# GroupNorm statistics of two residual sums from accumulating additions and ScalarE's squares instead of VectorE's bn_stats

## The chip, the cores and the metric

The kernel runs on one core of one Trainium2 chip. A core has TensorE (PE, matrix products), VectorE (DVE), ScalarE (ACT), GpSimd (POOL) and SyncE (SP, which here only issues DMAs); each works through its own queue of instructions in order, and they wait for each other by semaphores. The metric is the device time of one execution in microseconds, of which the median of several runs counts.

## The reference, cut to what matters

Four layers run one after the other on x of 16 x 32 x 128 x 128 fp32 (batch, channels, rows, columns). Each takes the GroupNorm of x (16 groups of two channels) and adds its result to x.

```
def _gn(v, G=16, eps=1e-5):
    g = v.reshape(B_, G, C_ // G, H_, W_)
    m = jnp.mean(g, axis=(2, 3, 4), keepdims=True)
    s = jnp.var(g, axis=(2, 3, 4), keepdims=True)
    return ((g - m) / jnp.sqrt(s + eps)).reshape(v.shape)
...
x = x + _L0_conv_ref(_gn(x), ...)    # a scan of LSTM cells over 128 columns
x = x + _L1_conv_ref(_gn(x), ...)    # quantised; out = -sum over c,kh,kw of |patch - w|
x = x + _L2_conv_ref(_gn(x), ...)    # Hartley transform, 32 x 32 modes mixed over channels, back
x = x + _L3_conv_ref(_gn(x), ...)    # five edge filters, seven 3x3 convolutions, three upsamplings
```

The means and variances that layers 2 and 3 need are those of x after layer 1 and after layer 2. This is what the change computes in another way.

## The kernel before, in words

**Stage 0** (`stage0`, to about 687 us) is layer 0. It already takes the statistics of its own result, for layer 1, from additions with a sum (L191, a custom VectorE operation followed by a read of the accumulator) and from squares on ScalarE (L198, with an accumulator read).

**The front** (`Differences.run`, L682) is layer 1. Work goes by half images: 16 batches x 2 halves, each a unit of 72 *differences* (8 output groups x 9 taps). A difference is max(q - w, 0) over a tile of 128 x 8192 fp16, made either by VectorE (L760, tile `d_dve`, three buffers) or by ScalarE (L757, tile `d_act`, two buffers). TensorE adds each up over partitions into four PSUM banks (`sums`, L647, 16 matmuls of 512 columns), together with a linear part (L662) and, where the plan leaves it idle, matmuls with zeros (`keep_busy`, L677). When a unit is complete, `finish` (L624) adds the four banks to the residual `xr1` (four scalar_tensor_tensor, L628), takes bn_stats of each (L630), and later stores the sum as x2 (eight DMAs).

**The background** (`After`) is layers 2 and 3. It works on groups of four batches. Group g starts when batch 4g+3 has been finished: `scaling` (L1149) aggregates the bn_stats of its four batches; `forward` does the Hartley transform (L1107 to L1083), reflects and mixes the modes (L1218); `back` (L1245) transforms back (L1292, L1342) and in 16 steps adds the result to the residual (`take_out`: two scalar_tensor_tensor, L1317, two bn_stats, L1320), which lies in `xr2` in a ring of four buffers: a step is stored as x3, and the buffer is loaded again for the step four later (`residual`, L1261). After the last step `back` aggregates the 32 bn_stats (L1359) and forms the mean and scale of layer 3 (`normalised`, L780). Then come the filters' statistics (L1488), conv1 (L1871), the small layers (L1661, L908) and the last layer (`last`, L1923, additions at L1993).

**The order of the work** is written out ahead by a planner, `Weave`, and kept as it stands (`keep_order`). The planner carries a clock for each engine, `weave.dve`, `weave.act` and `weave.pe`, to which each step adds its cost (`DVE_US, ACT_US, PE_US = 2.36, 7.15, 0.88` for a difference on VectorE, on ScalarE, and its sums on TensorE). Each next difference goes to the engine that would end it first (L742 to L749). Steps put off with `later(us, step)` are issued when the plan's time has reached them; `summed(step)` puts one off until after the matmuls planned so far; `done(v)` issues one at once if it still waits. A negative number that a generator yields is a distance that the plan keeps before the next step.

Groups 0 to 2 run in the background of the front. What is left of group 2, and all of group 3, run in **the tail**, where `drain` (L455) interleaves the two. Group 3 has the whole image in SBUF (`self.whole`), so that its way back adds in place and neither stores nor reloads.

Of the kernel before, what the change touches and what calls it, by code (L numbers as in the profile page):

```python
# [333 lines left out]
def by_rows(nc, tile, dram, store=False):  # L334

    for j in range(4):
        part = tile[32 * j : 32 * j + 32]
        rows = bass.AP(dram.tensor, dram.offset + j * dram.ap[0][0], [list(v) for v in dram.ap[1:]])
        if store:
            nc.sync.dma_start(rows, part)  # L340
        else:
            nc.sync.dma_start(part, rows)


def jc_rows(t, b, half, at=0, rows=16):

    first = t.offset + b * CHW + (64 * half + at) * W
    return bass.AP(t.tensor, first, [[16 * W, 4], [HW, C], [1, rows * W]])


class Weave:
# [103 lines left out]
def drain(*weaves):  # L455

    live = list(weaves)
    for w in live:
        w.draining, w.stretch = True, 1.5
    while live:  # L460
        w = min(live, key=lambda w: w.now)
        us = w.step()
        w.now = max(w.now + (us or 0.0), w.until)
        w.due(float("inf") if us is None else w.now)
        if us is None:
            live.remove(w)
            for w in live:
                w.alone, w.stretch = True, 1.0


def keep_order(nc, tc, start):

    last = {}
    for i in nc.cur_bb.bb.instructions[start:]:
        if i.engine in last:
            tc.add_manual_dep(
                i,
                last[i.engine].name,
                mybir.DependencyInfo(mybir.DependencyClass.NoSync, mybir.DependencyReason.DATA),
                reason="order",  # L480
            )
        last[i.engine] = i

DVE_US, ACT_US, PE_US = 2.36, 7.15, 0.88
LATE, ACT_SPARE = 1.5, 1.5
SLACK, CLOCK = 1.0, 1.0
# [3 lines left out]
def rest(nc, tc, cst, sel16, bias, m1, r1, a, d, out):  # L493


    with ExitStack() as ctx:
        sm = ctx.enter_context(tc.tile_pool(name="s1_sm", bufs=1))
        stat = sm.tile([128, B, 8, 6], F32, name="stat2")
        with tc.tile_pool(name="s1_ps0", bufs=2, space=PSUM) as ps:
            first = Differences(nc, sm, ps, cst, sel16, m1, r1, a["adder_w"], d, stat)  # L500
        bg = ctx.enter_context(tc.tile_pool(name="b_ps", bufs=4, space=PSUM))
        after = After(nc, tc, "left", sm, bg, cst, bias, a, d, stat, out)
        weave = after.weave = Weave(after.work(range(NG - 1)))
        start = len(nc.cur_bb.bb.instructions)
        with ExitStack() as front:
            first.run(tc, front, weave)
        keep_order(nc, tc, start)

        end = copy.copy(after)
        end.side, end.ps = "right", ctx.enter_context(tc.tile_pool(name="c_ps", bufs=4, space=PSUM))  # L510
        end.spare, end.whole = bg, True

        end.buffers = {"t_x": 8, "xm": 8, "xw": 4, "t_w": 6, "t_r": 8, "frames": 3, "gm": 5, "e_v": 6, "l_x": 4}
        end.weave = Weave(end.work([NG - 1]))
        end.weave.now = end.weave.base = weave.now
        end.weave.finished = B - 1
        drain(weave, end.weave)


class Differences:  # L520
# [103 lines left out]
    def finish(self, b, half, acc, xr, **_):  # L624
        nc = self.nc
        v = [xr[k // 2][:, 512 * (k % 2) : 512 * (k % 2) + 512] for k in range(4)]
        for k in range(4):
            nc.vector.scalar_tensor_tensor(v[k], acc[k], self.sumw, v[k], ALU.subtract, ALU.add)  # L628
        for k in range(4):
            nc.vector.bn_stats(self.stat[:, b, 4 * half + k, :], v[k])  # L630

        def store():
            for i in range(2):
                by_rows(nc, xr[i], jc_rows(self.d["x2"], b, half, 8 * i, 8), True)
            if half:
                self.weave.finished = b

        start = max(self.weave.dve, self.weave.pe)
        self.weave.pe, self.weave.dve = start + 2.6, start + 5.6
        self.weave.later(max(self.weave.dve - self.weave.base, 0.0) + 0.5, store)  # L640

    def sums(self, acc, d, i, first, last):
# [320 lines left out]
class After:  # L963
# [185 lines left out]
    def scaling(self, g, pool):  # L1149

        nc, cst, weave = self.nc, self.cst, self.weave
        mr = self.sm.tile([128, 2, 4, C], F32, name="mr", bufs=2)
        mv = pool.tile([128, 4, 2], F32, name="mv2")
        for i in range(4):
            nc.vector.bn_aggr(mv[:, i, :], self.stat[:, 4 * g + i].rearrange("p a b -> p (a b)"))
        both = pool.tile([128, 2, 4], F32, name="both2")
        yield from normalised(nc, pool, self.ps, weave, mv, 4, cst["avg8_jc"], 1e-5, both)

        diag = pool.tile([32, 8, C], F32, name="diag")
        nc.vector.tensor_tensor(  # L1160
            diag, bcast(cst["ident"][:32, :], 1, 8), bcast(both[:32].rearrange("p a b -> p (a b)"), 2, C), ALU.mult
        )
# [82 lines left out]
    def back(self, g, load):  # L1245


        nc, tc, cst, d, weave = self.nc, self.tc, self.cst, self.d, self.weave
# [3 lines left out]
        with self.pool("t_z") as zp_, self.pool("t_r", ahead) as rp:  # L1252
# [10 lines left out]
            def in_place(n, r):  # L1263

                row = 2 + 64 * (n % 2) + 32 * r + 4 * (n // 2)
                return self.image[:, row : row + 4, 2 : W + 2]

            xr = []
            stat = zp_.tile([128, 32, 6], F32, name="stat3")
            zi = zp_.tile([128, 32, 32], F32, name="zi")  # L1270
            for blk in range(4):
                first = z_d.offset + (4 * g + blk) * 32768
# [13 lines left out]
            for oh in range(2):  # L1286
                pa = [self.acc() for _ in range(4)]
                for o in range(16):
                    for r in range(4):
                        for blk in range(4):  # L1290
# [5 lines left out]
                                start=True,  # L1296
# [13 lines left out]
            def take_out(n, pf):  # L1310
                while ready.get(n):
                    weave.done(ready[n])
                for r in range(2):
                    v, p = xr[n][:, r] if not self.whole else in_place(n, r), pf[r]
                    if self.whole:
                        p = p.rearrange("p (r w) -> p r w", w=W)
                    nc.vector.scalar_tensor_tensor(v, p, 2.0**-15, v, ALU.mult, ALU.add)  # L1317
                for r in range(2):
                    v = xr[n][:, r] if not self.whole else in_place(n, r)
                    nc.vector.bn_stats(stat[:, 2 * n + r, :], v)  # L1320
                weave.dve += 2.8
                if self.whole:
                    return

                def store():
                    nc.sync.dma_start(rows(n)(x3), xr[n])
                    ready[n + ahead] = weave.later(6.0, lambda: reload(n + ahead)) if n + ahead < 16 else None

                ready[n + ahead] = weave.later(4.0, store)

            def reload(n):
                residual(n)
                ready[n] = None

            previous = None
            for n in range(16):
                s, half = n // 2, n % 2
                pf = [self.acc() for _ in range(2)]
                for i in range(4):
                    for r in range(2):  # L1340
# [5 lines left out]
                            start=True,  # L1346
# [8 lines left out]
            take_out(*previous)  # L1355
            if not self.whole:
                weave.later(7.0, lambda: [load(ch, half) for ch in range(self.buffers["frames"]) for half in range(2)])
            mv = zp_.tile([128, 1, 2], F32, name="mv3")
            nc.vector.bn_aggr(mv[:, 0, :], stat.rearrange("p a b -> p (a b)"))  # L1359
            yield from normalised(nc, zp_, self.ps, weave, mv, 1, cst["avg2_bc"], 1e-5, self.stats3)  # L1360
            nc.vector.scalar_tensor_tensor(
                self.shift3, self.stats3[:, 0], -1.0, self.stats3[:, 1], ALU.mult, ALU.mult
# [804 lines left out]
```

## Time and profile before

| | us |
|---|---|
| median of three runs | 6466.08 (6465.73 to 6471.06) |
| the profiled execution | 6473.52 |
| its span in the trace | 6471.7 |
| first difference starts, last sums end | 687.3, 5630 |
| VectorE, ScalarE, TensorE busy over the span | 5455.2, 5276.5, 5326.5 |
| differences on VectorE, on ScalarE | 1674, 630 |
| bn_stats at L630 and at L1320 | 128 and 128 |

The profile comes from one execution. Times are us, and those of single instructions often ns. An instruction's duration can overlap the next one's start on the same engine by about 0.1 us, so two equal instructions in a row tell their cost better by the distance between their starts. A wait is put down to what ended it last. "Idle before" in a group's row is the engine's idle time just before instructions of the group. In the list of differences by shape, 8192 and 8320 columns are two tilings of the same work.

### The profile page before, as it was taken

The numbers are of one execution on the slowest core, as the hardware profiler recorded it, in microseconds if no ns is written. First come the engines' busy times: TensorE is split into PE (matmuls) and PEld (weight loads), VectorE is DVE, ScalarE is ACT, GpSimd is POOL, SyncE is SP. The second block draws the span as 40 slices with busy tenths as digits, with TensorE's granted clock in tenths as the row PEclk, the third lists the DMA queues.
The fourth block names the chain that finished last, engine by engine and source line by source line (L and its number), as shares of the span: only waits on it lengthen the run. The fifth ranks groups of instructions, "written<-read, shape, count | busy, mean of one in ns | idle before, by whom it ended". The sixth has DMA issues, their size and how long they took to land.

```text
span 6471.7 us, 275922 instructions
## 1 busy us (share of the span) xinstructions
PE 5326.5 (82%) x130160; PEld 2805.8 (43%) x130160; DVE 5455.2 (84%) x6528; ACT 5276.5 (82%) x2779; POOL 58.7 (1%) x67
## 2 busy tenths in 40 slices
PE   3689577788877879998877879998888699977696
PEld 3576233344434433334443433334344333345594
DVE  7899899999999989999999889999999899834212
ACT  3899799999999989999999879999999899702001
POOL 0000000000000000000000000000000000000000
PEclk9999899999999989999999989999999899977898
DMA  7643313121154633222455532323455522344102
GB/s 313 222 178 125 87 48 84 48 57 45 32 138 124 204 117 88 64 72 73 142 147 150 168 93 58 97 51 102 129 144 179 162 58 63 97 131 137 33 4 65
DMA packets 363701, 700.94 MB, mean 108 GB/s; under 512 B 67972, under 2 KB 216452, under 8 KB 351684
## 3 DMA queue, kind: packets, MB, share of 16 engines
q1 hardware_dynamic: 355092, 648.86, 33.6%
q0 software_dynamic: 7040, 33.80, 1.6%
q8 instruction: 1018, 16.68, 1.1%
q14 instruction: 119, 0.97, 0.1%
q10 hardware_dynamic: 432, 0.64, 0.0%
HBM read 500.46 MB, written 182.69 MB: 106 GB/s over the span
## 4 chain that ended last, share of the span: by engine, by line
PE 26%; issue 11%; DVE 8%; ACT 3%; DMA 2%; SPq 0%; POOL 0%; DVEq 0%; ACTq 0%; POOLq 0%
PE acc L1871 10%; PE acc L647 9%; DVE d_dve L760 4%; PE acc L908 3%; ACT d_act L757 2%; PE acc L1661 1%; PE acc L1488 1%; PE acc L1292 1%; DMA xm_d<-xm 0%; PE acc L1218 0%; PE acc L662 0%; DVE pooled L1764 0%; PE acc L934 0%; DMA v<-fold_d 0%; PE acc L1844 0%
## 5 line engine op out<-in xcount | busy, mean ns | idle before, releaser
L757 ACT ACTIVATE d_act<-q,neg 128x8192 f16<-128x8192 f16 (+1 forms) x630 | 4463.6, 7152 | 215.9 <-PE acc L647 197.4
L760 DVE TENSOR_SCALAR d_dve<-q,qw 128x8192 f16<-128x8192 f16 (+1 forms) x1674 | 3868.3, 2360 | 215.3 <-PE acc L647 193.1
L647 PE MATMUL acc<-d_dve,sel 128*32 128x512 f16 x26784 | 1850.6, 395 | 409.4 <-DVE d_dve L760 305.6
L647 PEld LDWEIGHTS <-sel 128*32 128x32 f16 x36864 | 983.9, 99 | 1934.0 <-issue 1265.0
L647 PE MATMUL acc<-d_act,sel 128*32 128x512 f16 x10080 | 708.5, 401 | 147.9 <-ACT d_act L757 140.8
L1871 PE MATMUL acc<-xp,wf 32*32 32x512 f32 x19200 | 725.4, 607 | 23.0 <-issue 21.5
L677 PE MATMUL acc<-q,zero 128*32 128x512 f16 x8396 | 576.7, 390 | 7.1 <-issue 7.0
L223 PE MATMUL pg<-h,wb 64*64 64x20 f32 (+15 forms) x8192 | 341.3, 304 | 61.6 <-DVE h L251 34.8
L908 PE MATMUL acc<-y,u_conv 32*32 32x256 f32 x10752 | 318.4, 435 | 60.7 <-issue 45.1
L237 ACT ACTIVATE gt<-pg,bias 128x20 f32<-128x20 f32 (+15 forms) x1024 | 331.5, 383 | 41.6 <-PE pg L223 39.7
L1871 PEld LDWEIGHTS acc<-xp,wf 32*32 32x32 f32 x19200 | 222.4, 103 | 329.2 <-issue 297.9
L677 PEld LDWEIGHTS <-zero 128*32 128x32 f16 x8396 | 243.6, 99 | 228.1 <-issue 40.6
L1789 ACT ACTIVATE y<-pooled,b 128x128 f32<-128x128 f32 x112 | 39.5, 395 | 368.3 <-DVE pooled L1764 235.0
L223 PEld LDWEIGHTS pg<-h,wb 64*64 64x64 f32 x8192 | 251.4, 150 | 136.4 <-DVE h L251 81.5
L908 PEld LDWEIGHTS acc<-y,u_conv 32*32 32x32 f32 x10752 | 157.0, 110 | 164.3 <-issue 122.8
L1871 PE MATMUL acc<-image,wf 32*32 32x512 f32 x6400 | 207.8, 605 | 0.1
L223 PE MATMUL pg<-xn,wb 64*64 64x2 f32 (+63 forms) x4096 | 184.5, 290 | 25.9 <-issue 17.9
L1871 PEld LDWEIGHTS acc<-image,wf 32*32 32x32 f32 x6400 | 184.8, 103 | 20.3 <-issue 4.6
L1488 PE MATMUL acc<-xp 32*64 32x204 f32 (+2 forms) x6432 | 174.2, 338 | 15.8 <-issue 15.8
L1905 DVE TENSOR_TENSOR acc<-acc,cut 128x8 f32<-128x8 f32 x128 | 19.4, 166 | 193.4 <-PE acc L1871 193.1
L1661 PE MATMUL acc<-y,w_conv 32*32 32x512 f32 (+2 forms) x4608 | 144.3, 481 | 30.3 <-issue 18.0
L662 PE MATMUL acc<-q,sel 32*32 32x512 f16 x4608 | 158.4, 393 | 4.0 <-issue 4.0
(242 smaller groups left out, 3725.9 us busy)
## 6 DMA issues: line engine op xcount, KB each, us to landing
q<-q_d SPq DMA_DIRECT2D x128, 536.2 KB, 10.2
xp<-xn_d SPq DMA_DIRECT2D x24, 2112.0 KB, 9.1
x_in<-in_x_dram SPq DMA_DIRECT2D x16, 2048.0 KB, 14.7
xn<-in_xs_dram SPq DMA_DIRECT2D x64, 512.0 KB, 7.0
res<-in_x_dram SPq DMA_DIRECT2D x64, 512.0 KB, 8.9
x_d<-res SPq DMA_DIRECT2D x64, 512.0 KB, 4.6
xq<-x_d SPq DMA_DIRECT2D x256, 128.0 KB, 4.4
xr<-x_d SPq DMA_DIRECT2D x256, 128.0 KB, 4.3
```

Source lines behind the costliest of these rows:

```text
L223: nc.tensor.matmul(bank[c][q][64 * pair : 64 * pair + 64, :, :width], wb[half, 4 * kind + KIND[q]].rearrange("p b o -> p (b o)"), v[half], ...
L237: nc.scalar.activation(gt[:, q, :, :n], bank[c][q][:, :, :n], AF.Tanh if q == G else AF.Sigmoid, bias=bias[:, KIND[q] : KIND[q] + 1],)
L647: self.nc.tensor.matmul(acc[k][32 * j : 32 * j + 32, :], self.sel16[:, i // 9, :], d[:, row : row + 4, c : c + W], start=first, stop=last,)
L662: self.nc.tensor.matmul(acc[k][32 * j : 32 * j + 32, :], self.sel16[rows, 8, :], q[rows, row : row + 4, kw : kw + W], start=False, stop=False,
L677: self.nc.tensor.matmul(acc[k][32 * j : 32 * j + 32, :], self.zero, q[:, :4, :W], start=False, stop=False)
L757: nc.scalar.activation(dst, src, AF.Relu, bias=self.neg[:, i : i + 1])
L760: nc.vector.tensor_scalar(dst, src, self.qw[:, i : i + 1], 0.0, ALU.subtract, ALU.max)
L908: nc.tensor.matmul(acc[blk][32 * j : 32 * j + 32, o : o + rows * n], t[part, 4 * par + tap, :], own[:, top : top + rows, left : left + n], ...
L1292: nc.tensor.matmul(pa[blk][32 * r : 32 * r + 32, 32 * o : 32 * o + 32], zi[part, 16 * oh + o, :], cst["cas_t"][part, 32 * r : 32 * r + 32] ...
L1488: nc.tensor.matmul(gram[blk][j : j + width, at : at + n], xp[part, l, 2 + j : 2 + j + width], xp[part, rows, j : j + width + 4], start=sta ...
L1661: nc.tensor.matmul(acc[blk][32 * j : 32 * j + 32, : rows * n], wc[name][part, tap, :], pick(part, blk, j)[:, tap // 3 : tap // 3 + rows, t ...
L1871: nc.tensor.matmul(acc[blk][32 * j : 32 * j + 32, :], tap_of("all", tap)[rows], xp[rows, at + apart * j + kh : at + apart * j + kh + 4, kw ...
```

## The change

bn_stats and bn_aggr give way to a class `Sums` in two places: the sums of layer 1 (`finish`, for `scaling`) and those of the way back (`take_out`, for layer 3).

- The additions at L628 and L1317 give the sum of their result as well (`accum_out`, a column of `total`).
- After the first half of a batch, and after the first step of a way back, `centre` makes a number near the mean, from the first block of 512: minus its mean, in `away`.
- ScalarE squares each block about that centre (`square`: Square with `away` as bias, its sum in a column of `squared`, the result itself in a tile that nobody reads). In `finish` the squares are put off until 0.5 us after the plan's end of the additions; in the way back with `summed`.
- `moments` makes mean and variance from the two: two reductions and four small operations, in place of four aggregations in `scaling` or one in `back`. In `back` all squares still put off are issued first, and a distance of 2.5 is kept.
- The planner's costs change with it: 3.4 for the finish on VectorE (it was 5.6) and 3.9 on ScalarE, 1.6 for a step of the way back (it was 2.8) and 2.0 on ScalarE.

Everything else, the layers' arithmetic included, stays. Since the plan deals the differences out by its clocks, the order of the instructions on all engines is a new one.

```
+class Sums:
+    def __init__(self, nc, pool, groups, blocks, junk, name):
+        self.nc, self.groups, self.blocks = nc, groups, blocks
+        self.total = pool.tile([128, groups, blocks, 1], F32, name=f"total{name}")
+        self.squared = pool.tile([128, groups, blocks, 1], F32, name=f"squared{name}")
+        self.away, self.junk = pool.tile([128, groups], F32, name=f"away{name}"), junk
+
+    def centre(self, g):
+        self.nc.vector.tensor_scalar(self.away[:, g : g + 1], self.total[:, g, 0], -1.0 / 512, None, ALU.mult)
+
+    def square(self, g, k, v):
+        self.nc.scalar.activation(
+            self.junk if len(v.shape) == 2 else self.junk.rearrange("p (r w) -> p r w", w=W),
+            v, AF.Square, bias=self.away[:, g : g + 1], accum_out=self.squared[:, g, k],
+        )
+
+    def moments(self, pool, lo, hi):
+        nc, n = self.nc, hi - lo
+        mv, t = pool.tile([128, n, 2], F32, name="mv"), pool.tile([128, n], F32, name="mv_t")
+        nc.vector.tensor_reduce(mv[:, :, 0], self.total[:, lo:hi].rearrange("p g k a -> p g (k a)"), AX.X, ALU.add)
+        nc.vector.tensor_reduce(mv[:, :, 1], self.squared[:, lo:hi].rearrange("p g k a -> p g (k a)"), AX.X, ALU.add)
+        nc.vector.tensor_scalar(mv, mv, 1.0 / (512 * self.blocks), None, ALU.mult)
+        nc.vector.tensor_add(t, mv[:, :, 0], self.away[:, lo:hi])
+        nc.vector.tensor_mul(t, t, t)
+        nc.vector.tensor_sub(mv[:, :, 1], mv[:, :, 1], t)
+        return mv
...
@@ finish @@
         for k in range(4):
-            nc.vector.scalar_tensor_tensor(v[k], acc[k], self.sumw, v[k], ALU.subtract, ALU.add)
-        for k in range(4):
-            nc.vector.bn_stats(self.stat[:, b, 4 * half + k, :], v[k])
+            nc.vector.scalar_tensor_tensor(
+                v[k], acc[k], self.sumw, v[k], ALU.subtract, ALU.add, accum_out=self.stat.total[:, b, 4 * half + k]
+            )
+        if half == 0:
+            self.stat.centre(b)
+
+        def squares():
+            for k in range(4):
+                self.stat.square(b, 4 * half + k, v[k])
+            self.weave.act += 3.9
...
-        self.weave.pe, self.weave.dve = start + 2.6, start + 5.6
+        self.weave.pe, self.weave.dve = start + 2.6, start + 3.4
+        self.weave.later(max(self.weave.dve - self.weave.base, 0.0) + 0.5, squares)
         self.weave.later(max(self.weave.dve - self.weave.base, 0.0) + 0.5, store)
...
@@ scaling @@
-        mv = pool.tile([128, 4, 2], F32, name="mv2")
-        for i in range(4):
-            nc.vector.bn_aggr(mv[:, i, :], self.stat[:, 4 * g + i].rearrange("p a b -> p (a b)"))
+        mv = self.stat.moments(pool, 4 * g, 4 * g + 4)
...
@@ take_out, in back @@
-                    nc.vector.scalar_tensor_tensor(v, p, 2.0**-15, v, ALU.mult, ALU.add)
-                for r in range(2):
-                    v = xr[n][:, r] if not self.whole else in_place(n, r)
-                    nc.vector.bn_stats(stat[:, 2 * n + r, :], v)
-                weave.dve += 2.8
+                    nc.vector.scalar_tensor_tensor(
+                        v, p, 2.0**-15, v, ALU.mult, ALU.add, accum_out=stat.total[:, 0, 2 * n + r]
+                    )
+                if n == 0:
+                    stat.centre(0)
+                weave.dve += 1.6
+
+                def square():
+                    for r in range(2):
+                        stat.square(0, 2 * n + r, xr[n][:, r] if not self.whole else in_place(n, r))
+                    weave.act += 2.0
+
+                squares.append(weave.summed(square))
...
@@ after the last step of back @@
-            mv = zp_.tile([128, 1, 2], F32, name="mv3")
-            nc.vector.bn_aggr(mv[:, 0, :], stat.rearrange("p a b -> p (a b)"))
+            for v in squares:
+                weave.done(v)
+            yield -2.5
+            mv = stat.moments(zp_, 0, 1)
             yield from normalised(nc, zp_, self.ps, weave, mv, 1, cst["avg2_bc"], 1e-5, self.stats3)
```

More of the change, by code (lines that the diff above doesn't have):

```diff
@@ L482, in keep_order @@
         last[i.engine] = i
+class Sums:
[9 more added lines that the diff above has]
+            self.junk if len(v.shape) == 2 else self.junk.rearrange("p (r w) -> p r w", w=W),
+            v,
+            AF.Square,
+            bias=self.away[:, g : g + 1],
+            accum_out=self.squared[:, g, k],
+        )
[9 more added lines that the diff above has]
+        return mv
 DVE_US, ACT_US, PE_US = 2.36, 7.15, 0.88
@@ L497, in rest @@
         sm = ctx.enter_context(tc.tile_pool(name="s1_sm", bufs=1))
-        stat = sm.tile([128, B, 8, 6], F32, name="stat2")
+        stat = Sums(nc, sm, B, 8, sm.tile([128, 512], F32, name="junk2"), "2")
         with tc.tile_pool(name="s1_ps0", bufs=2, space=PSUM) as ps:
@@ L1268, in back @@
             xr = []
-            stat = zp_.tile([128, 32, 6], F32, name="stat3")
+            stat, squares = Sums(nc, zp_, 1, 32, self.stat.junk, "3"), []
             zi = zp_.tile([128, 32, 32], F32, name="zi")
```

## The prediction

> **What bounds the kernel now.** I read the page's busy line, then the busy time in two stretches (the front, from the first difference to the last sums, 687 to 5630 us, and the tail after it), then the groups of instructions by shape on VectorE and ScalarE, then waits and start times.
>
> ```profile
> PE 5326.5 (82%) x130160; PEld 2805.8 (43%) x130160; DVE 5455.2 (84%) x6528; ACT 5276.5 (82%) x2779; POOL 58.7 (1%) x67
> ```
>
> ```profile
> core 0: us, PE busy (x) PEld busy (x) DVE busy (x) ACT busy (x) POOL busy (x), PEclk, DMA share, GB/s
> 687.30:5630.00 4942.70, 4211.12 (x95376) 1942.07 (x95377) 4645.17 (x3816) 4681.33 (x974) 49.75 (x48) 0.95 0.35 99
> 5630.00:6471.70 841.70, 651.59 (x22493) 489.05 (x22475) 248.47 (x662) 81.85 (x132) 6.52 (x13) 0.83 0.27 83
> ```
>
> Over the span no engine looks like the bound. In the front it is VectorE and ScalarE together: 4645 and 4681 of 4943 us. They share 2304 differences (L757, L760), dealt out by the plan. In the tail both are nearly idle, and the chain of waits is TensorE's convolutions.
>
> ```profile
> L760 DVE TENSOR_SCALAR d_dve<-q,qw 128x8192 f16<-128x8192 f16 x1100 | 2556.3, 2349 | 142.0 <-PE acc L647 121.5 <-DMA co_c<-in_conv_dram 16.3
> L628 DVE SCALAR_TENSOR_TENSOR xr<-acc,sumw,xr 128x512 f32<-128x512 f32 x128 | 87.1, 745 | 11.4 <-PE acc L647 11.4
> L630 DVE BATCH_NORM_STATS2 stat<-xr 128x6 f32<-128x512 f32 x128 | 78.9, 680 | 0.0
> L1317 DVE SCALAR_TENSOR_TENSOR xr<-acc,xr 128x512 f32<-128x512 f32 x96 | 61.5, 683 | 1.3 <-PE acc L1342 1.3
> L1320 DVE BATCH_NORM_STATS2 stat<-xr 128x6 f32<-128x512 f32 x96 | 61.3, 680 | 0.0
> L191 DVE DVE_READ_ACCUMULATOR2_ANT sums<- 128x1 f32 x248 | 20.4, 82 | 0.0
> ```
>
> ```profile
> L757 ACT ACTIVATE d_act<-q,neg 128x8192 f16<-128x8192 f16 x436 | 3085.8, 7121 | 174.2 <-PE acc L647 155.8 <-DMA co_c<-in_conv_dram 18.1
> L198 ACT ACTIVATE junk<-res,away 128x512 f32<-128x512 f32 x128 | 95.3, 744 | 1.3 <-DVE sums L191 1.2
> L198 ACT ACTIVATION_READ_ACCUMULATOR junk<-res,away 128x1 f32 x128 | 28.4, 222 | 0.0
> ```
>
> L630 and L1320 are what the change removes; L191 and L198, in the first stage, already do what it adds. Durations overlap, so I cost by the distance between starts:
>
> ```profile
> 644.13 0.69 DVE L191 CUSTOM_DVE_ANT_1 res<-res,h 128x512 f32<-128x512 f32 x1
> 644.74 0.69 DVE L191 CUSTOM_DVE_ANT_1 res<-res,h 128x512 f32<-128x512 f32 x1
> ```
>
> ```profile
> 645.15 0.72 ACT L198 ACTIVATE junk<-res,away 128x512 f32<-128x512 f32 x1
> 646.00 0.72 ACT L198 ACTIVATE junk<-res,away 128x512 f32<-128x512 f32 x1
> ```
>
> An addition with its sum takes 0.61 us, a square with its sum 0.85 us. By the same reading of the timeline a bn_stats takes 0.60 us (pairs start 1.20 apart), a difference 2.27 us on VectorE and 7.07 us on ScalarE.
>
> ```profile
> ACT d_act L757 <- PE acc L647: 197.4, 85, 28.6
> DVE d_dve L760 <- PE acc L647: 193.1, 172, 6.6
> ```
>
> ```profile
> DMA to landing us min/median/max: 3.6/4.7/12.4
> ```
>
> Each engine loses some 200 us of the front to buffers that TensorE has not yet freed; that loss I first leave as it is. The last line is for the reloads of `xr2` (L1261).
>
> [...] The changed program holds as many table loads as before, three (the trace has 1.28 us for one), so I take none. [...] an accumulating scalar_tensor_tensor is in no row before.
>
> **The change part by part.** Of 256 changed additions, 224 lie in the front (128 at L628, 96 of three groups at L1317), 32 in the tail.
>
> *VectorE, front.* bn_stats removed: 224 x 0.60 = -134.4 us. Reads of accumulators: +0.01 each by L191, at most +0.12 by the loop at L1557 (0.64 between starts, 0.52 from start to read); I take 0.03: +6.7, ends 2 and 27. Centres: 19 x 0.2 = +3.8, by the spacing of small operations in the timeline. Moments: six small operations (1.2 us) for four aggregations (1.05 us) or one (1.02 us): nothing, and one more engine is waited for, named below.
>
> *ScalarE, front.* Squares: 224 x 0.847 = +189.7 us.
>
> *The deal.* The built program gives VectorE 1706 differences (1674 before) and ScalarE 598 (630): +32 x 2.27 = +72.6 and -32 x 7.07 = -226.2. Sums: VectorE -134.4 + 6.7 + 3.8 + 72.6 = -51.3 us, ScalarE +189.7 - 226.2 = -36.5 us. Both are the bound, so the front gains between the two: -44 us.
>
> *What is given back in the front.* A square waits for its addition (new on ScalarE). Queued behind it are differences that TensorE adds up in order. 80 sets of squares; the plan puts them 0.5 us or more behind VectorE, and behind a difference already under way, 3.5 us more on average. I take one set in five late by 1.3 us (TensorE's own waits for ScalarE at L647 are 140.8 us in 105): 80/5 x 1.3 = 21, of which three quarters fall into idle time: +5, ends 0 and 25. Around conv1 TensorE is the third bound (from 5200 to 5630 it is busy 419 of 430 us). A third of the front is like that, and some of the finish's gain, about 0.8 us net for each of 32 halves, goes there: +3, ends 0 and 9.
>
> *The reloads.* Stores of `xr2` stay where they were on SP, but the reload into the same buffer now waits for the squares too; behind it on SP stand the loads of q and xq. Before, a buffer came round in 18.6 us (additions of four steps, 4.65 apart) and needed 11: store landed 5, reload 4.7, addition 1.3. By the order of the programs this loop is tighter after the change: 39, 39 and 41 differences long in the three groups, where it was 52, 48 and 49, and a reload stands mostly 1 to 3 VectorE differences ahead of its addition (2 to 5 before). I work the new pace out as 4.4 us per step (ScalarE: 0.4 of a difference, 2.8, and two squares, 1.7), so 17.6 per round, against a need of 11 to 15. It just fits: +4, ends 0 and 90 (36 reloads at 2.5).
>
> Front: -44 + 5 + 3 + 4 = -32 us.
>
> *Tail.* Group 2's conv1 is 368 matmuls further when the last difference is issued (448 left before, 80 after): 23 rounds of 16 at 0.62 us (the unbroken conv1 in the chain: 4519 matmuls in 175.8 us) = -14.3, on the path, since TensorE is busy 38.9 of the first 47 us and 41 of the next 43. The loop over group 3's sums (5869 to 5922) is VectorE's now (46.7 of 54 us); it loses 32 x 0.6 = 19 us, but TensorE is busy 49.3 there with group 2's last layer: -5. Against it: squares behind the last addition and the moments, +1; the second matmul of the statistics now stands behind 108 more matmuls at 0.039, +4; the new distances that the plan sets at this place, +1. Tail: -13, ends -30 and +5. Nothing moves on POOL; its loads wait for the same shift.
>
> Sum: -45 us. Against the profiled execution (6473.5 us, of which 6471.7 are span): 6428.5. The median of the runs is 7.4 lower, 6466.1; so **6421 us**.
>
> **The rivals.**
> *It gives all.* Squares and reloads find their slots, and the tail gets the end it could: -48 (54.6 differences' worth saved on VectorE, 26.8 spent on ScalarE, at 0.58 per us) - 28 = 6390. For it: 261 us of idle ScalarE in the front. Against: that idle time is made by TensorE's order, not free for use.
> *The time stays.* The front is held by TensorE's order and the planner's idle slots; the filler matmuls (L677) rise from 8396 to 8804, which says that TensorE waits more, not less. Front -10, tail +4: 6460.
> *Slower, by the reloads.* The reload waits for the squares, VectorE waits for the reload, ScalarE's next squares wait for VectorE, and TensorE for both. 36 reloads; from 1.4 us each (49 us, the sum without it) the gain is gone; at 2.5 us each, half a landing, it is 90 - 49 = +41: 6507. For it: the short lead in the order. Against: before, no idle of VectorE is put down to these reloads.
> *Slower, by the accumulator.* [...] It decides from 0.23 us per addition. Against: L191 and L1557.
>
> **How the numbers follow.** Chances: forecast 0.50 (own range 6405 to 6440), all 0.20, stays 0.18, reloads 0.06, accumulator 0.06. 0.2% is 13 us, about what a measurement of this kernel can tell from no change. Faster than 6453: 0.50 + 0.19 + 0.05 = 0.74. Within: 0.12, nearly all from "stays". Slower: 0.12 + 0.02 = 0.14. The range leaves out about 0.08 below and 0.12 above: 6385 to 6475.
>
> **What would show it.** Right: the additions with their reads start 0.61 to 0.70 us apart; squares 0.85; the last difference ends about 32 us earlier, near 5598; VectorE busy some 50 us less in the front and ScalarE some 35. Wrong: idle time of VectorE before the additions of the way back that ends with a DMA (reloads); additions of over 0.9 us (accumulator); a wait of ScalarE for the additions of over 40 us in all; or a front that is no shorter while VectorE and ScalarE idle more behind L647 (stays).

## The result, and the profile after

| | before | after |
|---|---|---|
| median of 20 runs each | 6466.7 us (6456.5 to 6484.0) | 6453.2 us (6439.7 to 6465.9) |
| ratio after / before | | 0.9979, 95% interval 0.9971 to 0.9987 |
| profiled execution | 6473.5 us | 6445.4 us |
| front: 687 us to the first addition of the last half image | 4940.4 us | 4951.6 us |
| tail: from there to the end | 844.3 us | 804.9 us |

The change makes the kernel faster by 13.5 us (8 to 19 by the interval), a third of the 45 that were forecast. The two profiled executions differ by 28; they lie 7 above and 8 below their medians. Against the forecast "front -32, tail -13", the front is 11 us *longer* and the tail 39 shorter.

The changed kernel's busy line, and its busy time in these two stretches (the columns are those of the table by stretch in the prediction):

```profile
PE 5328.1 (83%) x130568; PEld 2806.8 (44%) x130568; DVE 5378.5 (83%) x6608; ACT 5257.7 (82%) x3259; POOL 66.9 (1%) x67
```

```profile
687.00:5638.60 4951.60, 4251.50 (x96449) 1957.58 (x96452) 4589.46 (x3892) 4634.35 (x1386) 56.57 (x45) 0.95 0.35 99
5638.60:6443.50 804.90, 610.29 (x21818) 471.82 (x21810) 226.68 (x665) 108.78 (x200) 7.95 (x15) 0.83 0.29 87
```

The front of the kernel before, up to the same point (its tail has TensorE busy 654.2 us in 22554 matmuls):

```profile
687.00:5627.40 4940.40, 4208.52 (x95302) 1940.94 (x95305) 4642.58 (x3812) 4681.33 (x974) 48.32 (x45) 0.95 0.35 99
```

So the front lost 53 us of VectorE's work and 47 of ScalarE's, near the forecast (51 and 37), and isn't shorter: VectorE idles 362 us of it where it idled 298, ScalarE 317 where it idled 259. And TensorE does 43 us *more* in it. Two things make this up: 736 matmuls that stood in the tail are now made in the front, and 408 more with zeros are put in (8396 to 8804 in all, 28 us of busy time in their row). The 736 are all conv1 (L1871, now L1923) of group 2, as its rows in the two tails show, before and after:

```profile
L1871 PE MATMUL acc<-xp,wf 32*32 32x512 f32 x896 | 37.5, 622 | 8.1 <-issue 8.1
L1923 PE MATMUL acc<-xp,wf 32*32 32x512 f32 x160 | 6.8, 689 | 0.0
```

Of VectorE's idle time, its wait for buffers that TensorE has not freed is this, where it was 193.1 us (ScalarE's stands with experiment 1):

```profile
DVE d_dve L804 <- PE acc L691: 222.8, 179, 7.3
```

The two stretches aren't two separate sums. What the front makes less of, the tail makes more of.

The prices of the new instructions, in the groups by shape (after the bar: busy time and mean duration, then the idle time ahead of them and what ended it):

```profile
L664 DVE SCALAR_TENSOR_TENSOR xr<-acc,sumw,xr 128x512 f32<-128x512 f32 x128 | 88.4, 748 | 26.9 <-PE acc L691 25.8 <-ACT d_act L801 1.1
L664 DVE DVE_READ_ACCUMULATOR xr<-acc,sumw,xr 128x1 f32 x128 | 10.9, 85 | 0.0
L1359 DVE SCALAR_TENSOR_TENSOR xr<-acc,xr 128x512 f32<-128x512 f32 x96 | 62.2, 685 | 9.7 <-DMA xr<-x_d 9.1 <-issue 0.5
L502 ACT ACTIVATE junk<-xr,away 128x512 f32<-128x512 f32 x224 | 161.8, 722 | 91.9 <-DVE away L499 55.3 <-DVE xr L664 13.8 <-DVE xr L1359 12.4
L502 ACT ACTIVATION_READ_ACCUMULATOR junk<-xr,away 128x1 f32 x224 | 41.9, 187 | 0.0
```

An addition with its sum lasts what it lasted without (748 against 745 ns, 685 against 683). The reload of `xr2` is waited for 9.1 us in all. The timeline of VectorE in the way back shows what the read of a sum costs:

```profile
2061.53 0.68 DVE L1359 SCALAR_TENSOR_TENSOR xr<-acc,xr 128x512 f32<-128x512 f32 x1
2062.13 0.08 DVE L1359 DVE_READ_ACCUMULATOR xr<-acc,xr 128x1 f32 x1
2062.13 0.69 DVE L1359 SCALAR_TENSOR_TENSOR xr<-acc,xr 128x512 f32<-128x512 f32 x1
```

The next addition starts 0.60 us after the first, together with the read: it lies beside the next instruction. Two additions of the way back take 1.21 us here, from the first start to that of the instruction behind them, where two without a sum took 1.19 to 1.20, so that the sum costs about a hundredth of a us each. What is new and large is in the row of the squares: ScalarE stands idle 91.9 us ahead of them. The longest stretch of it, on ScalarE, and VectorE's timeline at that place:

```profile
2294.03 7.12 ACT L801 ACTIVATE d_act<-q,neg 128x8192 f16<-128x8192 f16 x1
2325.79 0.72 ACT L502 ACTIVATE junk<-xr,away 128x512 f32<-128x512 f32 x1 [24.65 <-DVE away L499]
```

```profile
2298.84 1.71 DVE L1679 SCALAR_TENSOR_TENSOR wf<-v,ops,wf 128x1440 f32<-128x1440 f32 x1
2302.96 5.36 DVE L1679 SCALAR_TENSOR_TENSOR wf<-v,ops,wf 128x1152 f32<-128x1152 f32 x5 [2.41 <-DMA v<-fold_d]
...
2317.76 1.85 DVE L1679 SCALAR_TENSOR_TENSOR wf<-v,ops,wf 128x1152 f32<-128x1152 f32 x2 [1.27 <-DMA v<-fold_d]
```

The row names the centre, but the centre isn't what is slow. The plan let all 15 folds of the tables (L1677, L1679) go out between two differences, their loads are waited for in between, and the addition, its centre and ScalarE's squares stand behind them. The kernel before has such a bunch too, but in another group, with no square behind it.

### The profile page after: what moved, and what is told of

Read it like the earlier page. It is cut to its first block, busy times and chain, and to the rows that moved or that the text cites. A ratio compares the mean times of both kernels' runs of the same rounds, so it can differ in the third digit from the quotient of the medians.

```text
span 6443.5 us, 277540 instructions
## 1 busy us (share of the span) xinstructions
PE 5328.1 (83%) x130568; PEld 2806.8 (44%) x130568; DVE 5378.5 (83%) x6608; ACT 5257.7 (82%) x3259; POOL 66.9 (1%) x67
## 4 chain that ended last, share of the span: by engine, by line
PE 39%; issue 14%; DVE 9%; ACT 3%; DMA 2%; SPq 0%; POOL 0%; DVEq 0%; ACTq 0%; POOLq 0%
PE acc L691 15%; PE acc L1923 13%; DVE d_dve L804 5%; PE acc L952 3%; ACT d_act L801 2%; PE acc L1540 2%; PE acc L1713 1%; PE acc L721 1%; PE acc L706 1%; PE acc L1896 1%; PE acc L1260 1%; PE acc L978 1%; DMA v<-fold_d 1%; PE acc L1334 0%; DVE pooled L1816 0%
## 5 line engine op out<-in xcount | busy, mean ns | idle before, releaser
L801 ACT ACTIVATE d_act<-q,neg 128x8192 f16<-128x8192 f16 (+1 forms) x598 | 4241.8, 7149 | 176.8 <-PE acc L691 158.2
L804 DVE TENSOR_SCALAR d_dve<-q,qw 128x8192 f16<-128x8192 f16 (+1 forms) x1706 | 3941.3, 2361 | 242.8 <-PE acc L691 222.8
L691 PE MATMUL acc<-d_dve,sel 128*32 128x512 f16 x27296 | 1885.4, 395 | 375.2 <-DVE d_dve L804 258.3
L691 PE MATMUL acc<-d_act,sel 128*32 128x512 f16 x9568 | 667.2, 399 | 156.3 <-ACT d_act L801 139.5
L1923 PE MATMUL acc<-xp,wf 32*32 32x512 f32 x19200 | 725.7, 610 | 7.6 <-issue 5.8
L721 PE MATMUL acc<-q,zero 128*32 128x512 f16 x8804 | 604.3, 391 | 5.8 <-issue 5.8
L721 PEld LDWEIGHTS <-zero 128*32 128x32 f16 x8804 | 257.2, 99 | 237.6 <-issue 41.3
L1923 PEld LDWEIGHTS acc<-xp,wf 32*32 32x32 f32 x19200 | 217.8, 103 | 312.9 <-issue 281.8
L502 ACT ACTIVATE junk<-xr,away 128x512 f32<-128x512 f32 x224 | 161.8, 722 | 91.9 <-DVE away L499 55.3
L1923 PE MATMUL acc<-image,wf 32*32 32x512 f32 x6400 | 207.0, 603 | 0.0
L1923 PEld LDWEIGHTS acc<-image,wf 32*32 32x32 f32 x6400 | 179.3, 103 | 24.9 <-issue 3.7
```

Of the source, the lines that this page charges most:

```text
L502: self.nc.scalar.activation(self.junk if len(v.shape) == 2 else self.junk.rearrange("p (r w) -> p r w", w=W), v, AF.Square, bias=self.away ...
L691: self.nc.tensor.matmul(acc[k][32 * j : 32 * j + 32, :], self.sel16[:, i // 9, :], d[:, row : row + 4, c : c + W], start=first, stop=last,)
L721: self.nc.tensor.matmul(acc[k][32 * j : 32 * j + 32, :], self.zero, q[:, :4, :W], start=False, stop=False)
L801: nc.scalar.activation(dst, src, AF.Relu, bias=self.neg[:, i : i + 1])
L804: nc.vector.tensor_scalar(dst, src, self.qw[:, i : i + 1], 0.0, ALU.subtract, ALU.max)
L1923: nc.tensor.matmul(acc[blk][32 * j : 32 * j + 32, :], tap_of("all", tap)[rows], xp[rows, at + apart * j + kh : at + apart * j + kh + 4, kw ...
```

## The experiments

Three theories stood at the start. *Waits*: the squares' new waits ate the gain. *TensorE*: where conv1 fills TensorE, nothing can be gained. *Order*: the plan that comes out with the new costs is a different order of the same work, good or bad by chance. Each kernel ran beside the kernel before on the same chip; ratios are to it, with their 95% intervals.

**1. Squares that needn't wait.** The order of the changed kernel, with squares that read constants:

```diff
+        one = self.ready[:, :1]
...
+        v = bass.AP(one.tensor, one.offset, [list(one.ap[0])] + dims)
         self.nc.scalar.activation(
...
             AF.Square,
-            bias=self.away[:, g : g + 1],
+            bias=one,
+            scale=100.0,
```

> Same plan and same order as the changed kernel; only the squares read a column of ones (scale 100, bias 1) in place of the sum and the centre, so ScalarE no longer waits for an addition, and a tile's reload no longer waits for a square. Leaves out the true second moment: the statistics of the residual's sums and of the way back are those of constants. Theory 1 (the new waits of ScalarE, 92 us of idle time in the trace, ate the gain of the front): 6395 to 6420 us, the front (687 to the last difference) 35 to 50 us shorter than the changed kernel's 4956. Theory 2 (the order of the plan and TensorE hold the front, the waits only stand where ScalarE would have waited for TensorE anyway): 6440 to 6460 us, the idle time of ScalarE ahead of its differences grows by what goes ahead of the squares.

Measured: 6440.4 us, 0.9963 (0.9950 to 0.9975), some 10 to 13 us below the changed kernel (10 by the ratios, barely clear of their noise). The waits cost something, but a seventh to a ninth of what stood in the row. ScalarE's waits for TensorE ahead of its differences show where the rest is: first the changed kernel, then this one (us, times, longest).

```profile
ACT d_act L801 <- PE acc L691: 158.2, 90, 13.8
```

```profile
ACT d_act L806 <- PE acc L696: 203.7, 92, 37.6
```

Of the idle time that left the squares, 46 us came back ahead of the differences: ScalarE only arrived earlier at a buffer that wasn't free yet. ScalarE's idle time in the front fell by 19 us, from 317 to 298. The time lies at the lower edge of what *TensorE* forecast, and half of the idle time moved where it said.

**2. And moments that needn't wait.**

```diff
+        nc.gpsimd.memset(self.squared, 5e6)
...
-            accum_out=self.squared[:, g, k],
+            accum_out=self.spare,
```

> As the kernel with ready squares, and the reduction of the squares reads a tile set once by GpSimd, so VectorE doesn't wait for ScalarE before the moments either (13 us of idle time in the trace, 4 waits). Leaves out the second moment in the same way. Theory 1: 5 to 12 us below the kernel with ready squares. Theory 2: the same as that kernel within 4 us.

Measured: 6439.0 us, 0.9963 (0.9949 to 0.9977). VectorE's waits for the squares cost nothing that can be measured.

**3 and 4. One half of the change alone.** In the residual's sums (`finish`) only, and in the way back (`take_out`) only; the other place keeps its bn_stats.

> The change in the residual's sums alone; the way back keeps bn_stats. By the sum of the prediction: 128 of the 224 statistics, VectorE -77 +4 and ScalarE +109 over the front, balanced by about 18 moved differences: -21 us of the -44, no tail gain: 6445. Theory 1: the waits of the residual's squares (a third of the 92 us) leave -5 to -15 against before: 6450 to 6460. Theory 2 (TensorE-bound stages and the order decide): within 8 us of before, and the rest of the changed kernel's gain is from the tail.

> The change in the way back alone; the residual's sums keep bn_stats (their tile holds 8 images in turn). By the sum of the prediction: 96 of the 224 statistics, -16 us in the front and -13 in the tail: 6437. Theory 1: the way back's squares stall ScalarE most (an addition waits for its own matmuls): the front gains nothing or loses 5 to 10, the tail -13 or more: 6450 to 6460. Theory 2: the front within 10 us of before on either side by the order's luck.

Measured: 6454.5 us, 0.9983 (0.9976 to 0.9991), and 6468.4 us, 1.0002 (0.9992 to 1.0012). Both are 10 to 30 us behind their parts of the sum. Read alone, they say that the way back gains nothing. The pairs below show why that isn't a safe reading: each of these is one order.

**5 and 6. The bunch of folds taken apart, in both kernels.**

```diff
                 if len(v) < 10:
                     table()
-                yield -1.2
+                yield -4.0
```

> The changed kernel with the fold of the tables spread out: 4.0 in place of 1.2 us of planned time after each of its 10 steps, so that its 15 instructions no longer go out in one piece in group 0 (where ScalarE idled 24.7 us behind them). Nothing is left out. Theory of the bunch: 15 to 25 us below the changed kernel: 6428 to 6438. Theory of TensorE's work (the sum of TensorE's busy time sets the end where conv1 runs, and a stall ahead of it is made up by it): within 6 us of the changed kernel: 6447 to 6459.

> The kernel before with the same spreading of the fold, whose 15 instructions went out in one piece in its group 1. Nothing is left out. Theory of the bunch: 15 to 30 us below the kernel before: 6437 to 6451, so that the change's own effect between the two spread kernels stays at about -13. If only the changed kernel suffered from its bunch, this one stays at 6466 and the change's own effect between the two spread kernels is -35.

Measured: the changed kernel 6443.3 us, 0.9966 (0.9953 to 0.9979), 10 better (8 by the ratios, whose intervals overlap), less than forecast; the kernel before 6496.1 us, 1.0047 (1.0034 to 1.0060), 31 *worse*. The theory of the bunch has the wrong sign there. In the changed kernel the bunch lies in the eleventh half image (2297 to 2320 us), and that half image is 23 to 25 us shorter in each complete order measured without the bunch (experiments 5, 10, 12, 16 and 18); in experiments 5, 10 and 12 more than half of that is lost again by the end. But the change, between two kernels that are spread alike, is now worth 53 us, not 13. The two stretches of the spread kernel before, and of the spread changed one:

```profile
687.00:5574.40 4887.40, 4162.61 (x93904) 1957.18 (x93907) 4629.98 (x3796) 4674.51 (x966) 99.21 (x45) 0.95 0.35 99
5574.40:6488.70 914.30, 729.84 (x24634) 516.63 (x24626) 256.34 (x681) 85.13 (x140) 7.95 (x15) 0.86 0.26 81
```

```profile
687.00:5591.30 4904.30, 4245.51 (x95638) 1969.41 (x95641) 4582.35 (x3884) 4640.43 (x1383) 94.03 (x45) 0.95 0.35 100
5591.30:6450.00 858.70, 669.35 (x23066) 498.05 (x23058) 230.10 (x673) 111.04 (x204) 7.95 (x15) 0.83 0.27 82
```

The spread kernel before has a front 53 us shorter than the one before, and leaves 2080 more matmuls to the tail, which is 70 us longer. A shorter front is no gain by itself: what counts is front and tail together.

**7 and 8. Room on TensorE.** Both spread kernels with 14 of conv1's 25 taps.

```diff
-            for tap in range(25):
+            for tap in [t for t in range(25) if t % 2 == 0 or t == 23]:
```

> The kernel before, spread, with 14 of conv1's 25 taps (leaves out the other 11: 1408 matmuls of 512 columns a group, about 85 us of TensorE a group at 0.0605 each). TensorE then has room in all of the front; the tail, which is one group's chain, falls by about 85: 6360 to 6390. It serves as the base of the next one.

> The changed kernel, spread, with 14 of conv1's 25 taps (leaves out the other 11). TensorE theory (what VectorE and ScalarE save is not seen where conv1's matmuls fill TensorE, 10 of the front's 32 units): with room on TensorE the change is worth 30 to 45 us against its base with the same taps. Theory of the waits (the squares' waits ate it): it is worth 10 to 18 us, as with all taps.

Measured: 6244.7 us (0.9660, 0.9647 to 0.9672) and 6210.5 us (0.9603, 0.9590 to 0.9615): the change is worth 34 us. Where group 3's conv1 runs unbroken, the trace of the kernel before has up to 651 records in 20 us, two for a matmul: 0.061 us each, near the 0.0605 of the expectation. But the base fell by far more than the 85 us forecast, since now nothing of the first three groups is left for the tail: in both traces the last layer of the third ends before the front does (at 5602 and 5541 us). Base first, then the changed one:

```profile
687.00:5628.60 4941.60, 4164.90 (x94155) 1993.55 (x94158) 4675.53 (x3936) 4735.03 (x1007) 103.42 (x45) 0.94 0.36 103
5628.60:6240.10 611.50, 387.49 (x13970) 316.90 (x13962) 198.77 (x536) 58.91 (x104) 7.94 (x15) 0.77 0.28 82
```

```profile
687.00:5594.50 4907.50, 4164.77 (x94850) 1999.63 (x94853) 4627.89 (x4011) 4664.66 (x1412) 86.42 (x45) 0.95 0.36 103
5594.50:6209.60 615.10, 383.07 (x13970) 315.16 (x13962) 177.60 (x544) 88.29 (x176) 7.94 (x15) 0.77 0.28 82
```

Both tails hold the same 13970 matmuls, and the gain is where the prediction put it: the front 34 us shorter (forecast 32), the tail 4 longer (forecast, without its conv1 term, +1). This is close to the sum of the prediction, in a kernel in which nothing passes from front to tail. It is one pair, and there is luck in so close a fit: the plan moved 35 differences here, not 32, VectorE lost 48 us of work and ScalarE 70, and their idle time rose by 14 and 36.

**9 and 10. A third order.** Both kernels with 2.0 in place of 1.2 in the line of experiments 5 and 6. By then I had a fourth theory, of the *backlog*: that the background's chain of one group after the other sets the end, and the front's engines don't.

> The kernel before with 2.0 in place of 1.2 us of planned time after each step of the fold: a third plan of the same work, all taps, nothing left out. With the next one it gives the change's effect under a third order. Theory of the backlog (the background's chain of one group after the other, some 1390 us each whichever kernel, is not done when the front ends, and what is left goes to the tail): 6470 to 6500, by how far the chain of group 0 is put off. Theory of the order's luck alone: anything between 6450 and 6500.

> The changed kernel with the same 2.0. Backlog: worth less than the 34 us of the half taps against its base unless the base's chain is put off, 6440 to 6460, and in both traces the time from the first way back to the second stays at 1370 to 1410 us if the orders are alike. Order's luck alone: the change's effect scatters about -33 (so far -13 and -53 with all taps): 15 to 50 below its base.

Measured: 6496.9 us, 1.0047 (1.0035 to 1.0060), and 6450.0 us, 0.9972 (0.9961 to 0.9982): 47 us apart. Both lie within the backlog's ranges, but the time from the first way back to the second, forecast at 1370 to 1410 us in both, is 1445 us in the kernel before and 1358 in the changed one.

**11. No squares at all.**

```diff
-        self.weave.later(max(self.weave.dve - self.weave.base, 0.0) + 0.5, squares)
...
-                squares.append(weave.summed(square))
```

> The changed kernel without its 256 squares and without their planned cost (leaves the second moments out: they are constants). ScalarE is freed of 190 us in the front, 23 differences go back to it: some 45 us off both engines, and no wait for an addition, worth 13 alone. If VectorE and ScalarE set the end (the sum of the prediction carried on): 45 below the kernel with ready squares, 6395. Backlog: 29 of the 45 us lie in units 10 to 32, where the background's chain decides; only the units 1 to 9 and the tail's 6 us count: 6420 to 6435.

Measured: 6390.4 us, 0.9880 (0.9864 to 0.9896): 50 below the ready squares, and 30 below what the backlog allowed. The fronts of the two, ready squares first:

```profile
687.00:5621.30 4934.30, 4245.85 (x96450) 1957.11 (x96453) 4588.90 (x3893) 4636.45 (x1393) 55.26 (x45) 0.95 0.35 99
687.00:5538.50 4851.50, 4215.19 (x95570) 1962.93 (x95573) 4534.65 (x3862) 4622.96 (x965) 51.49 (x48) 0.95 0.36 101
```

The front is 83 us shorter and the tail 39 longer. The plan expected 45 us less on both engines; in the trace VectorE has 54 us less and ScalarE 14, and ScalarE idles 69 us less. So the result speaks against the backlog, but it doesn't show that work on VectorE and ScalarE counts one for one: the order is new here too, and the bunch of folds, which the kernel with ready squares has, is gone. Against the ready squares in another order (experiment 17, 6401.0 us) it is only 11 to 15 us better.

**12. Late squares.**

```diff
-        self.weave.later(max(self.weave.dve - self.weave.base, 0.0) + 0.5, squares)
+        self.weave.later(max(self.weave.dve - self.weave.base, 0.0) + 6.0, squares)
...
-                squares.append(weave.summed(square))
+                squares.append(weave.later(weave.lag() + 4.0, square))
...
-            yield -2.5
+            yield -7.0
             mv = stat.moments(zp_, 0, 1)
```

> The changed kernel with its squares put 4 to 5.5 us later in the plan, so that ScalarE finds sum and centre ready, and the moments of the way back 7 us behind the last piece in place of 2.5. Nothing is left out. The fold's bunch in group 0 is gone with it, by the new order. Theory 1 (waits, worth 13 by the kernel with ready squares): 6440 to 6446. Backlog: the same, if the chain of group 0 isn't put off; a later way back would cost 5 to 10 of it back: 6440 to 6455.

Measured: 6443.9 us, 0.9962 (0.9949 to 0.9975), some 10 better than the changed kernel, again with little room over the noise. Since its order differs too, it doesn't show by itself that the waits are what it gained.

**13 to 16. Two pairs that leave the folds alone.** In one, 11.0 in place of 12.0 us between a way back's loads and its first matmul (`yield -12.0` in `back`); in the other the planner's slack at 1.1:

```diff
-SLACK, CLOCK = 1.0, 1.0
+SLACK, CLOCK = 1.1, 1.0
```

> The kernel before with 11.0 in place of 12.0 us of planned time between the loads of a way back and its first matmul: the same work in a neighbouring order, nothing left out. Theory of the order (the order of the kernel before happens to be some 30 us better than its neighbours; the change itself is worth about 45): 6480 to 6500. Theory of a small effect (two slower neighbours were made slow by the spreading of the fold alone): 6460 to 6472.

> The changed kernel with the same 11.0. Both theories: 6440 to 6460; the effect against its base is 30 to 55 by the theory of the order, 5 to 20 by that of a small effect.

> The kernel before with the planner's slack at 1.1 in place of 1.0 us (how late a difference's sums may be made by background matmuls): again the same work in another order, with the fold paced as before. Theory of the order: 6480 to 6500. Theory of a small effect: 6460 to 6472.

> The changed kernel with the slack at 1.1. Both theories: 6440 to 6460, with the effect against its base as in the pair with 11.0: 30 to 55 by the theory of the order, 5 to 20 by that of a small effect.

Measured: 6462.3 (1.0000, 0.9991 to 1.0009) and 6434.8 us (0.9966, 0.9952 to 0.9979); 6474.1 (1.0027, 1.0015 to 1.0039) and 6408.0 us (0.9917, 0.9903 to 0.9930). Neither forecast of the bases holds in both: one didn't move (in the traces its half images take as long as the kernel before's within 6 us, in all but one of 32, so it is almost the same order), the other is 14 to 17 us worse. Both changed kernels came out below the 6440 to 6460 that both theories gave them. All pairs together; effects are from the ratios, times 6466; stretches and matmuls are from one profiled execution each, so that front and tail together can miss the effect by some 15 us:

| the same edit in both kernels | before | changed | effect, us | front | tail | matmuls in the tail |
|---|---|---|---|---|---|---|
| none | 1 | 0.9979 | -14 | +11 | -39 | -736 |
| 11.0 in the way back | 1.0000 | 0.9966 | -22 | +18 | -39 | -736 |
| fold at 2.0 | 1.0047 | 0.9972 | -48 | +10 | -57 | -1905 |
| fold at 4.0 | 1.0047 | 0.9966 | -52 | +17 | -56 | -1568 |
| slack at 1.1 | 1.0027 | 0.9917 | -71 | -30 | -45 | -872 |
| fold at 4.0, 14 taps | 0.9660 | 0.9603 | -37 | -34 | +4 | 0 |

The five with all taps have a mean of -41 us (spread 23, so some 10 either way for the mean). The second is hardly a draw of its own: its changed kernel too has almost the order of the first (within 5 us in all 32 half images). With these two taken as one, the mean is -47. The recorded pair is the least of them: of the five orders of the kernel before its own is the best, level with one that is nearly the same order, and of the five orders of the changed kernel its own is the worst, if by little.

**17 and 18. The slack at 1.1, with ready and with late squares.**

> The changed kernel with the slack at 1.1 and with squares of a column of ones in place of the sum and the centre (leaves the true second moment out): the same order as the changed kernel with the slack at 1.1, without the waits for additions. If the waits cost what they cost in the first order (13 us): 6395 against 6408. If the other order already hides them: within 5 of 6408.

> The changed kernel with the slack at 1.1 and the late squares, nothing left out: meant as a better version. If the two add up (-9 by late squares, -45 by this order): 6400. If an order is a draw of its own each time, as the scatter of the pairs says: 6405 to 6455, 6440 the likeliest.

Measured: 6401.0 us, 0.9904 (0.9891 to 0.9916), and 6419.1 us, 0.9934 (0.9917 to 0.9950). The waits cost 7 to 8 us in this order, not clear of the noise: the intervals overlap. Late squares, 10 better in one order, are 11 worse in this one, again with overlapping intervals: what a new order does is at least of the size of what the edit does. The best complete kernel of all is the changed one with the slack at 1.1: 6408 us, 0.8% below the kernel before.

## Why the prediction was wrong

- **The removed and added work: right, for ScalarE roughly.** VectorE -53 us in the front (forecast -51), ScalarE -47 (-37). Additions with a sum 0.60 to 0.61 us apart in the way back, squares 0.85. The rival of the slow accumulator, for which nothing in the trace of the kernel before spoke, is gone: 748 ns with the sum, 745 without.
- **The reloads: small, as forecast.** 9 us of idle VectorE in the changed kernel, forecast a cost of 4; this was not tested alone.
- **"I take one set in five late by 1.3 us": too small.** How many was right, how long wasn't: ScalarE waits 19 times for an addition or a centre, 4.3 us each on average, and once 24.6, as the timeline above shows, because the addition stands behind a whole piece of background work on VectorE. The idle time ahead of the squares is 92 us in all, not 21. What they cost was 10 to 13 us (7 to 8 in the other order), not 5.
- **"Each engine loses some 200 us of the front to buffers that TensorE has not yet freed; that loss I first leave as it is": this is the step that failed.** I never came back to it, and allowed 12 us in all for what is given back. The idle time of the front is no constant: it rose by 64 us on VectorE and 58 on ScalarE, more than the engines had saved. Only on VectorE did the wait for TensorE's buffers itself grow, from 193 to 223 us; on ScalarE it fell, from 197 to 158, and the 92 us ahead of the squares came on top. With it fell the next two lines, "front -32" (measured +11) and "tail -13" (measured -39). In all five pairs with all taps the tail is shorter, by 39 to 57 us; the front is longer in four of them. It is shorter with the slack at 1.1, by 30 us, and with conv1 cut down, where nothing is left over, by 34.
- **The tail's conv1 term: the count right, the price half, and nothing put in the front.** The program's loop has 3200 matmuls of conv1 in a group, the trace 6400 records of them, two for each. So the forecast's 368 (448 left before, 80 after), doubled, are the trace's 736 (896 and 160) exactly; but they were priced as 23 rounds, at 0.62 us for 16 *records*. At that price 46 rounds are 29 us, not 14.3 (the two rows of the tails differ by 30.7 us of busy time), and the forecast for the tail would have been -27. The same work then has to be made in the front, and there the sum puts nothing for it, although it counts TensorE as the third bound around conv1. Whether this is what lengthened the front stays open. The number alone doesn't do it: with the slack at 1.1, 872 matmuls moved, the idle time rose by only 18 and 23 us, and the front is shorter.
- **The size of the sum.** Forecast -45; measured -13.5 in this pair, -41 in the mean of five. The total was good for the change, with luck: the split of it, -32 in the front and -13 in the tail, holds in no pair with all taps. For the one pair of orders that was measured it was three times too large. I priced the new order at nothing, where the same edits of the plan, on unchanged work, move the kernel before by 0 to +31 us and the changed one by -4 to -40. That the order alone moves the time is shown (+30, +30 and +17 by the ratios in the kernel before, with intervals clear of 1). What makes one order good isn't: taking the bunch of folds apart goes with 10 us less in one kernel and 31 more in the other. In the kernel before, the time from the first way back to the second is 1457 us when the fold is spread and 1384 when it isn't, but why the background of that group falls so far behind, and whether this makes the 31, stays open.
- **"The time stays", at 6460, came nearest.** It had the front right in kind (no shorter, while the engines idle more), but not the tail (forecast +4, measured -39). Whether TensorE's order held this front stays open; with the slack at 1.1 and with conv1 cut down the front did become 30 and 34 us shorter.

## What to carry to other kernels

Where a planner places the work by its costs, a change of costs makes a new order, and one pair of orders measures the change plus a draw (here -14 to -71 us for a change worth some 40 to 50): put the same small, neutral edits of the plan into both versions and compare several pairs before you believe or drop a change of under 1%. Ahead of a tail that shares work with the front, forecast both stretches together, counting what is left over at the border, and don't carry the idle time over as a constant. Count what is moved in the same unit as its price: the program's instructions and the trace's records can differ. An idle time that the profile puts down to a wait isn't its price: here 92 us in the row were worth about 10.

## What was not expected of the hardware

- Executions of one program differ by more than the parts of the sum: 6439.7 to 6465.9 us in 20 runs of the changed kernel, so that a single profile of it is good to some 10 us.
- A matmul of conv1 (fp32, 512 columns) leaves two records in the trace: 6400 for the 3200 of a group.
- The read of VectorE's sum (83 to 85 ns in its rows) starts with the next addition and lies beside it, so that even the 0.03 us that were taken for it were too much. ScalarE's read of a square's sum (187 ns) isn't hidden between two squares: squares that last 0.72 us start 0.85 apart.
